# A two-layer graph network on one core: two weights are loaded later, the last pair is finished by halves of the features, and all end places are new

## The chip, the cores and the metric

The kernel runs on one core of a Trainium2 chip. A core has five engines that take their instructions in order, each from a queue of its own: TensorE (PE, matmuls), VectorE (DVE), ScalarE (ACT), GpSimd (POOL) and SyncE (SP, which here only issues DMAs). They meet through semaphores. The metric is the device time of one execution in microseconds (us).

## The reference

```python
x: (128 graphs, 128 nodes, 512 features), adj: (128, 128), all float32
# layer 0
q, k, v = (x @ Wq + bq, x @ Wk + bk, x @ Wv + bv), each in 8 heads of 64
scores = q @ k^T / sqrt(64) + (1 - adj) * -1e9
x = layernorm(x + softmax(scores) @ v @ Wo + bo)
# layer 1
h = x @ W;  s1 = h @ a1;  s2 = h @ a2
e = leaky_relu(s1[:, None] + s2[None, :], 0.2) * adj
h_prime = softmax(e) @ h
x = layernorm(x + elu(h_prime + beta * h))
```

Both norms have no scale and no shift of their own. The graphs do not touch each other.

## The kernel before

**Tiling.** The 128 graphs are taken two at a time: 64 pairs (G = 2, NG = 64), graph b0 and b1 of pair g. A pair brings 2 x 128 rows of 512 features. Everything is float32, and each matmul shows as two records in the trace.

**Block products.** q, k, v, w (the product with Wo) and h (the product of layer 1) are 2 x 2 block products done with seven block products instead of eight: `product(name, g, n)` with n from 1 to 7 (L269). It needs sums of weight blocks, made once by `weight_sum` (L207, on DVE for q and k, on POOL for v, w and h), and differences of data blocks for each pair, made by `block_sum` on POOL (L238). Products 1, 6, 5 and 3 go on in the same half of a PSUM bank (the main region), one on top of the other; 2 has the other half; 7 and 4 go to a side bank. After each of 1, 6, 5 and 3 `take_part` copies the state out (ACT for q, k, v and h, DVE for w), and the next product into that half waits for it. `add_block` (DVE) adds product 2, and the states after 7 and 4, to what take_part left. A block product of q or k is 4 matmuls of 128 columns, one of v, w or h 2 matmuls of 256 columns.

**Stages of a pair.** fetch_blocks and turn_x (DVE transposes x), block_sum x, q and k, scores (PE), mask (DVE), row_max (DVE), exps (ACT), row_inv, normalise (ACT), attn_write and attn_read (through DRAM, SP), turn_attn (DVE), v, attend (PE), attend_evict (ACT), w with the residual (x + bo, made by `residual` on POOL), the norm (bn_stats, bn_aggr, add_eps on DVE, inv_std on POOL), s1 and s2 by row_product (DVE), edge, leaky, edge_max, edge_exp, edge_inv, weights (the tile att), weights_write and weights_read through DRAM, weights_turn, aggregate (PE, tile pz), aggregate_evict (ACT, tile zT), h, then elu_max, elu_exp, elu_sum (u = max(h, 0) + x1, then + min(exp(h), 1)), the norm of layer 1, store. The -1 of elu falls away in the norm.

**The order is written out.** Nothing is scheduled by a tool. `rows(g)` (L685) gives every operation of a pair a place in us; pair g's places are shifted by g * STEP (36.678). `last_rows(g)` (L759) has the lists of the last two pairs; the table `other` has own places for pairs 0 to 3, NG - 4 and NG - 3. All pieces are sorted by place and emitted in that order, so the places decide only the order within each engine's queue, SP's and POOL's too:

```python
with tc.manual_schedule():
    for _, _, fn, args in sorted(pieces, key=lambda p: p[:2]):
        fn(*args)
```

Several pairs are under way at once: the operations of a pair spread from place -44 to 134.

**The start.** At the very beginning SP issues the blocks of pair 0, then wq, wk and wv (1 MB each, `load_turned`, L99), then, as their places come, the blocks of pair 1, the rows of x, wo and w1 (`load_weight`, L121). The biases, adj, a1, a2, beta and bo come on POOL's queue. `keep_busy(20, "early")` (L139) sets 20 idle products with the identity at the head of PE's queue.

**The end.** The last pair does w and h without block sums: `plain` (L323) does four matmuls of 512 columns into a bank for each graph; for this the free halves of wq_sb and wk_sb are loaded again with half of wo and of w1 (`load_again`). Six idle products ("late") stand in its list. Per graph follow elu_exp (ACT, L645), elu_max (DVE, L649), elu_sum (L654), bn_stats (L464), bn_aggr (L472), add_eps (L486), inv_std (POOL, L490), shift (L658), norm_f (ACT, L664) and store (L670), all over 512 features. The tile u has two buffers (`uf`).

## Time and profile before

| | |
|---|---|
| median of three runs | 2392.12 us (2390.34 to 2392.55) |
| the profiled execution | 2389.93 us |
| its span, first to last instruction | 2388.1 us |
| mean granted clock of PE | 0.997 |
| DMA traffic | 269.82 MB, 113 GB/s on average |
| wq, wk, wv landed at | 9.61, 12.99, 17.80 us |
| blocks of pair 1 landed by | 22.44 us |
| rows of x for pair 0 landed at | 22.4 and 23.12 us |
| last matmul ends at | 2379.43 us |

A share of busy time is a mean over the whole span. The table of windows gives the same by stretch of time: where PE is busy for the whole of a window, PE sets the pace there; where it isn't, the table of waits says what ended its pauses. A pause of another engine costs nothing by itself. The granted clock is a column of that table too: 1.00 is full speed. DVE's row of work in the page:

```profile
L387 DVE TENSOR_REDUCE nmax<-s 128x8 f32<-128x1024 f32 x128 | 153.5, 1199 | 2.3
L379 DVE SCALAR_TENSOR_TENSOR s<-psc,amask 128x512 f32<-128x512 f32 x256 | 167.6, 676 | 27.6 <-PE psc L371 27.3
L341 ACT COPY h<-ph 128x256 f32<-128x256 f32 x252 | 94.6, 376 | 258.4 <-PE ph L293 257.1
```

After the bar stand the busy sum, the mean duration of one in ns, and the idle time of the engine ahead of these instructions with what ended it.

### The profile page before, as it was taken

The page shows a single profiled execution, that of the slowest core. Times are in us where ns is not written, and L with a number is a line of the kernel's source. Part 1 is how long each engine was busy: PE and PEld are TensorE (multiplying, and loading weights), DVE is VectorE, ACT ScalarE, POOL GpSimd, SP SyncE. Part 2 cuts the span into 40 slices and gives each one's busy share as a digit, 9 for nine tenths or more (in the row PEclk, how much of TensorE's full clock was granted, in tenths as well). Part 3 has the DMA queues.
Part 4 walks back from the last instruction along what each step waited for, and adds up shares of the span by engine and source line. Part 5 has one row for each costly group of instructions (what it writes and reads, how often), then busy time and mean ns, then how long its engine had stood idle before and what let it go on. Part 6 is the DMA issues. An engine that isn't in the chain of part 4 may idle for free.

```text
span 2388.1 us, 50634 instructions
## 1 busy us (share of the span) xinstructions
PE 2359.0 (99%) x17708; PEld 2179.7 (91%) x17708; DVE 1876.4 (79%) x4381; ACT 1583.2 (66%) x5760; POOL 867.2 (36%) x1047
## 2 busy tenths in 40 slices
PE   8999999999999999999999999999999999999998
PEld 7898999999999999999999999999999999999985
DVE  6787787877877877878778778778788787787877
ACT  4676766766666666667666676676676666766655
POOL 6242433433433334334334333343343343333421
PEclk9999999999999999999999999999999999999999
DMA  6333334344343343343433433433434334334332
GB/s 191 103 95 115 108 104 132 92 120 124 101 119 114 103 125 105 106 132 93 120 121 103 119 112 105 125 100 111 133 91 120 117 107 118 107 111 125 118 100 73
DMA packets 255905, 269.82 MB, mean 113 GB/s; under 512 B 57425, under 2 KB 204369, under 8 KB 255265
## 3 DMA queue, kind: packets, MB, share of 16 engines
q1 hardware_dynamic: 254704, 265.45, 37.0%
q8 instruction: 140, 2.29, 0.4%
q14 instruction: 117, 0.95, 0.1%
q0 software_dynamic: 400, 0.86, 0.1%
q10 hardware_dynamic: 544, 0.26, 0.0%
HBM read 157.62 MB, written 108.85 MB: 112 GB/s over the span
## 4 chain that ended last, share of the span: by engine, by line
PE 95%; DMA 2%; DVE 1%; ACT 1%; SPq 0%; issue 0%; DVEq 0%; ACTq 0%
PE pv L293 12%; PE pk L299 12%; PE pq L299 11%; PE pw L293 11%; PE ph L293 11%; PE eq L299 9%; PE psc L371 5%; PE po L446 5%; PE pz L634 5%; PE ew L293 4%; PE ev L293 4%; PE eh L293 4%; DMA scr<-sb 1%; ACT sb L407 1%; DMA ab<-scr 1%; DMA wk_sb<-in_L_gnn_Wk_dram 0%
## 5 line engine op out<-in xcount | busy, mean ns | idle before, releaser
L393 ACT ACTIVATE s<-s,nmax 128x128 f32<-128x128 f32 x1024 | 398.1, 395 | 150.1 <-DVE nmax L387 150.1
L427 POOL TENSOR_TENSOR x<-x,bo_b_in 128x512 f32<-128x512 f32 x128 | 163.8, 1280 | 892.6 <-DMA x<-in_x_dram 769.9
L407 ACT ACTIVATE sb<-s,rinv 128x128 f32<-128x128 f32 x1024 | 319.5, 395 | 2.9 <-DMA scr<-sb 2.6
L347 ACT ACTIVATE kT<-pk,bk_c 128x128 f32<-128x128 f32 x512 | 160.6, 367 | 194.1 <-PE pk L299 151.5
L341 ACT COPY h<-ph 128x256 f32<-128x256 f32 x252 | 94.6, 376 | 258.4 <-PE ph L293 257.1
L347 ACT ACTIVATE qT<-pq,bq_c 128x128 f32<-128x128 f32 x512 | 159.2, 364 | 89.7 <-PE pq L299 89.3
L393 ACT ACTIVATION_READ_ACCUMULATOR s<-s,nmax 128x1 f32 x1024 | 196.9, 192 | 0.0
L252 POOL TENSOR_TENSOR th<-zT,zT 128x256 f32<-128x256 f32 x63 | 46.3, 736 | 395.5 <-ACT zT L641 395.5
L379 DVE SCALAR_TENSOR_TENSOR s<-psc,amask 128x512 f32<-128x512 f32 x256 | 167.6, 676 | 27.6 <-PE psc L371 27.3
L344 DVE TENSOR_TENSOR w<-pw,x 128x256 f32<-128x256 f32 x252 | 103.2, 410 | 101.0 <-PE pw L293 100.9
L497 DVE SCALAR_TENSOR_TENSOR ya<-w,wa_row 128x512 f32<-128x512 f32 x256 | 177.6, 694 | 4.4
L436 DVE STREAM_TRANSPOSE attnT<-ab 128x512 f32<-128x512 f32 x256 | 172.6, 694 | 7.4 <-DMA ab<-scr 6.5
L458 ACT ACTIVATE oT<-po,bv_c 128x128 f32<-128x128 f32 x512 | 139.6, 382 | 27.7 <-PE po L446 27.7
L387 DVE TENSOR_REDUCE nmax<-s 128x8 f32<-128x1024 f32 x128 | 153.5, 1199 | 2.3
L232 DVE STREAM_TRANSPOSE xT<-xblk 128x512 f32<-128x512 f32 x128 | 143.1, 1120 | 5.2 <-DMA xblk<-in_x_dram 5.2
L299 PEld LDWEIGHTS pk<-xT,wk_sb 128*128 128x128 f32 x1024 | 136.0, 195 | 10.6 <-issue 4.2
L299 PE MATMUL pk<-xT,wk_sb 128*128 128x128 f32 x1024 | 136.9, 278 | 4.1 <-DMA wk_sb<-in_L_gnn_Wk_dram 4.1
L293 PE MATMUL pv<-wv_sb,xT 128*128 128x256 f32 x512 | 137.6, 391 | 0.0
L299 PE MATMUL pq<-xT,wq_sb 128*128 128x128 f32 x1024 | 134.8, 275 | 0.0
L299 PEld LDWEIGHTS pq<-xT,wq_sb 128*128 128x128 f32 x1024 | 129.4, 192 | 3.3
L371 PE MATMUL psc<-kT,qT 64*128 64x128 f32 x2048 | 131.8, 278 | 0.0
L371 PEld LDWEIGHTS psc<-kT,qT 64*128 64x128 f32 x2048 | 119.4, 188 | 11.5 <-issue 11.3
(674 smaller groups left out, 6297.0 us busy)
## 6 DMA issues: line engine op xcount, KB each, us to landing
scr<-sb SPq DMA_DIRECT2D x128, 512.0 KB
ab<-scr SPq DMA_DIRECT2D x512, 128.0 KB
x<-in_x_dram SPq DMA_DIRECT2D x128, 256.0 KB
out_dram<-u SPq DMA_DIRECT2D x128, 256.0 KB
xblk<-in_x_dram SPq DMA_DIRECT2D x254, 128.0 KB
pb<-s2d SPq DMA_DIRECT2D x62, 128.0 KB
attd<-att SPq DMA_DIRECT2D x62, 128.0 KB
ab<-attd SPq DMA_DIRECT2D x248, 32.0 KB
```

Source lines behind the costliest of these rows:

```text
L232: nc.vector.transpose(xT[g][:, :, t * N : (t + 1) * N].rearrange("p m (b r) -> p b m r", r=Q), xblk[g][:, t].rearrange("p b (c m) -> p b m ...
L293: nc.tensor.matmul(out, b[:, c, :], a[:, c, :], start=first and c == 0, stop=(c == 1), skip_group_check=True,)
L299: nc.tensor.matmul(out[:, m * N : (m + 1) * N], a[:, c, m * P : (m + 1) * P], b[:, c, :], start=first and m == 0 and c == 0, stop=(c == 1) ...
L347: nc.scalar.activation(dst[:, m, :], src[:, m * N : (m + 1) * N], AF.Identity, bias=BIAS[name][:, 2 * i + m : 2 * i + m + 1],)
L371: nc.tensor.matmul(psc[b][j][:, m, :], qT[g][feats, m, rows], kT[g][feats, m, rows], start=True, stop=True,)
L379: nc.vector.scalar_tensor_tensor(s_t[b][:, j * HP : (j + 1) * HP, :], psc[b][j], SCALE, amask.rearrange("p (o n) -> p o n", o=1).broadcast ...
L387: nc.vector.tensor_reduce(nmax[b], s_t[b], AX.X, ALU.max, negate=True)
L393: nc.scalar.activation(s_t[b][:, h, :], s_t[b][:, h, :], AF.Exp, bias=nmax[b][:, h : h + 1], accum_out=rsum[b][:, h : h + 1],)
L407: nc.scalar.mul(sb[b][:, :, h, :], s_t[b][:, h, :].rearrange("p (b c) -> p b c", c=Q), rinv[b][:, h : h + 1],)
L427: nc.gpsimd.tensor_tensor(xr[b], xr[b], later["bo"], ALU.add)
L436: nc.vector.transpose(attnT[b].rearrange("p h (a r) -> p a h r", r=Q)[:, rows], ab[b].rearrange("p a (h c) -> p a h c", c=Q)[:, rows],)
L497: nc.vector.scalar_tensor_tensor(z, y[b], 1.0, wa_row[j], ALU.mult, ALU.mult, accum_out=s12[g][:, i, j : j + 1])
```

## The change

There are three parts.

1. **Start.** wk and wv are no longer issued right behind wq. A piece `load_k_and_v` stands at place 5.685, between the two turns of pair 0's x (5.683 and 6.713). Its memset of one column of wk_sb on DVE gives wk's DMA something on DVE to wait for, so that it issues behind the first turn. In pair 0 the q products stand ahead of the k products (before: k first), and DVE makes q's weight sums ahead of k's. w1 is loaded ahead of wo (before: behind), the rows of x of pair 0 ahead of the blocks of pair 1. There are 15 early idle products instead of 20.
2. **End.** In the last pair, layer 1's product, elu, statistics, norm and store work on halves of 256 features: half 1 ahead of half 0. The statistics of both halves go into one tile and are aggregated together; half 0 is normed by ACT, half 1 by DVE; there are four stores of 128 KB instead of two of 256 KB. The late idle products are gone. In the list of the last pair, graph b0's edges, weights, aggregate and product run ahead of b1's edge_max.
3. **Places.** All places are new: those of the steady pairs in rows(g), of the last two pairs, of the pairs in `other`, and of the single pieces at the start. The operations of a steady pair are the same, STEP too; in each queue their order is another. Among them, in a steady pair: row_max of b1 now stands ahead of add_block v 2 (before behind it), and take_part v 6 stands behind that add in both; the tile v is the same. residual of b0 stands ahead of the scores, before behind them. The number of matmuls that compute something does not change (halves apart: 16 of 256 columns instead of 8 of 512 in the last pair).

```diff
     load_turned(wq_sb, wq)
-    load_turned(wk_sb, wk)
-    load_turned(wv_sb, wv)
...
-    keep_busy(20, "early")
+    keep_busy(15, "early")
...
+    def load_k_and_v():
+        nc.vector.memset(wk_sb[:, 0, :1], 0.0)
+        load_turned(wk_sb, wk)
+        load_turned(wv_sb, wv)
...
+    def half(i):
+        return slice(i * HF, (i + 1) * HF)
+
+    def end_product(b, i):
+        pl["h", b, i] = ps_mm.tile([P, HF], F32, tag="mm", name=f"plh_{b}_{i}")
+        for c in range(NC):
+            nc.tensor.matmul(
+                pl["h", b, i], zT[b][:, c, :], (wk_sb if c < 2 else w1_sb)[:, c, half(i)],
+                start=(c == 0), stop=(c == NC - 1),
+            )
+
+    def end_exp(b, i):
+        nc.scalar.activation(whole("h", b)[:, half(i)], pl["h", b, i], AF.Exp)
+
+    def end_max(b, i):
+        if b not in u:
+            u[b] = wk2.tile([P, D], F32, tag="uf", name=f"u_{b}")
+        nc.vector.scalar_tensor_tensor(
+            u[b][:, half(i)], pl["h", b, i], 0.0, x1[b][:, half(i)], ALU.max, ALU.add
+        )
+
+    def end_sum(b, i):
+        nc.vector.scalar_tensor_tensor(
+            u[b][:, half(i)], hp[b][:, half(i)], 1.0, u[b][:, half(i)], ALU.min, ALU.add
+        )
+
+    def end_stats(b, i):
+        if b not in stats:
+            stats[b] = st.tile(
+                [P, 2, nc.vector.BN_STATS_DIM], F32, tag="stats2", name=f"stats2_{b}"
+            )
+        nc.vector.bn_stats(stats[b][:, i, :], u[b][:, half(i)])
...
+    def end_norm(b, i):
+        g, j = divmod(b, G)
+        dst, scale, bias = u[b][:, half(i)], rstd["f", g][:, j : j + 1], nmr[g][:, j : j + 1]
+        if i == 0:
+            nc.scalar.activation(dst, dst, AF.Identity, bias=bias, scale=scale)
+        else:
+            nc.vector.tensor_scalar(dst, dst, scale, bias, ALU.mult, ALU.add)
+
+    def end_store(b, i):
+        nc.sync.dma_start(out=out[b][:, half(i)], in_=u[b][:, half(i)])
...
     def rows(g):
...
-            (2.943, scores, b1), (3.203, product, "v", g, 1), (3.463, mask, b0, 0),
-            (3.487, mask, b0, 1), (3.658, row_max, b0), (4.555, exps, b0, 0),
-            (5.075, mask, b1, 0), (6.271, residual, b0), (6.383, product, "v", g, 2),
-            (6.541, exps, b0, 1), (7.568, take_part, "v", g, 1, 0, 0), (7.611, exps, b0, 2),
-            (8.122, product, "v", g, 7), (8.183, mask, b1, 1), (8.41, product, "v", g, 6),
-            (8.797, exps, b0, 3), (8.894, add_block, "v", g, 2, 0, 0),
-            (8.955, take_part, "v", g, 6, 1, 0), (9.854, row_inv, b0),
...
-            (11.052, row_max, b1), (11.513, normalise, b0, 3), (11.654, attn_write, b0),
-            (11.776, product, "v", g, 5), (12.497, exps, b1, 0), (13.24, exps, b1, 1),
...
+            (2.487, scores, b0), (3.199, scores, b1), (4.193, mask, b0, 0),
+            (4.492, product, "v", g, 1), (4.517, mask, b0, 1), (4.517, row_max, b0),
+            (4.641, mask, b1, 0), (5.302, take_part, "v", g, 1, 0, 0), (5.86, exps, b0, 0),
+            (6.834, residual, b1), (7.227, product, "v", g, 6), (7.65, product, "v", g, 2),
+            (7.788, exps, b0, 1), (8.282, mask, b1, 1), (8.312, exps, b0, 2),
+            (8.356, row_max, b1), (9.38, exps, b0, 3), (9.64, product, "v", g, 7),
+            (9.91, add_block, "v", g, 2, 0, 0), (10.078, take_part, "v", g, 6, 1, 0),
+            (10.336, row_inv, b0), (10.432, normalise, b0, 0), (10.446, normalise, b0, 1),
+            (10.513, normalise, b0, 2), (11.118, product, "v", g, 5), (12.165, normalise, b0, 3),
...
     def last_rows(g):
...
-            (43.463, keep_busy, 6, "late"), (43.587, weights, g, 0), (44.057, edge_max, g, 1),
...
-            (48.603, plain, "h", b0), (48.733, aggregate_evict, b1), (52.053, plain, "h", b1),
-            (53.543, elu_exp, b0), (55.613, elu_max, b0), (55.743, elu_exp, b1),
...
+            (46.907, aggregate_evict, b0), (47.677, end_product, b0, 1),
+            (49.407, end_product, b0, 0), (49.557, edge_max, g, 1), (49.647, end_exp, b0, 1),
...
+            (51.747, turn_weights, g, 1), (52.187, weights_evict, g, 1), (52.707, aggregate, b1),
+            (53.237, end_exp, b0, 0), (53.847, aggregate_evict, b1),
+            (54.617, end_product, b1, 1), (54.847, end_max, b0, 0), (55.207, end_max, b0, 1),
...
+            (58.317, end_max, b1, 0), (58.317, end_exp, b1, 0), (58.677, end_aggr, b0),
...
-    at(7.47, weight_sum, "k", 3, nc.vector)
...
-    at(10.35, weight_sum, "q", 3, nc.vector)
...
+    at(5.685, load_k_and_v)
+    at(8.723, weight_sum, "q", 3, nc.vector)
...
+    at(13.163, weight_sum, "k", 3, nc.vector)
```

## The prediction

> **What bounds the kernel now.** I read the page's busy line and chain first, then the table of windows for where TensorE (PE) stands still, then the waits of PE for what ends each pause, then the last microseconds, and last a stretch of VectorE's (DVE's) timeline in the middle.
>
> ```profile
> PE 2359.0 (99%) x17708; PEld 2179.7 (91%) x17708; DVE 1876.4 (79%) x4381; ACT 1583.2 (66%) x5760; POOL 867.2 (36%) x1047
> ...
> PE 95%; DMA 2%; DVE 1%; ACT 1%; SPq 0%; issue 0%; DVEq 0%; ACTq 0%
> ```
>
> PE is the bound. The diff adds and removes no real matmul, so only PE's pauses, its slow clock and what follows its last matmul can change.
>
> ```profile
> 0.00:20.00 20.00, 12.47 (x79) 12.15 (x80) 9.10 (x12) 2.54 (x5) 10.81 (x23) 0.91 0.93 264
> 200.00:220.00 20.00, 17.84 (x104) 16.20 (x103) 16.21 (x41) 16.32 (x62) 9.56 (x13) 0.94 0.32 111
> 1000.00:1100.00 100.00, 100.00 (x761) 92.70 (x761) 80.19 (x192) 69.90 (x257) 39.89 (x48) 1.00 0.33 102
> 2270.00:2290.00 20.00, 16.96 (x146) 15.60 (x146) 12.07 (x25) 7.76 (x27) 1.67 (x3) 0.91 0.21 66
> 2380.00:2388.10 8.10, 0.00 (x0) 0.00 (x0) 3.29 (x10) 1.69 (x3) 1.08 (x2) 0.61 0.17 65
> ```
>
> Columns: window, its length, busy time of PE, weight loads, DVE, ACT, POOL, then PE's granted clock, DMA share, GB/s. The middle is full (100 of 100); pauses lie in the first 100 us, near 217, near 2275, in the last pair and after the last matmul.
>
> ```profile
> PE pk L299 <- DMA wk_sb<-in_L_gnn_Wk_dram: 4.1, 1, 4.1
> PE ph L293 <- ACT h L341: 3.4, 4, 2.2
> PE pk L299 <- ACT kT L347: 3.0, 2, 1.9
> PE early L137 <- POOL ident masks.py:199: 2.7, 1, 2.7
> PE pq L299 <- ACT qT L347: 2.5, 1, 2.5
> ```
>
> ```profile
> 2379.53 0.61 ACT h L645
> ...
> 2384.22 0.81 ACT u L664
> ```
>
> Each wait line has the sum, how often, the longest (early is the idle product at the start). 4.1 us go by until wk is there; 2.5 (at 2279) and 2.2 (at 217) are single pauses. The two lines of the second fence are from the chain that ends last (start, us): behind the last matmul come exp at 2379.53, the norm at 2384.22, and the end at 2388.07.
>
> ```profile
> 1002.36 0.42 DVE L357 TENSOR_TENSOR kT<-eq,kT 128x256 f32<-128x256 f32 x1 [0.20 <-PE eq L299]
> 1002.70 0.42 DVE L357 TENSOR_TENSOR qT<-eq,qT 128x256 f32<-128x256 f32 x1
> 1003.03 1.13 DVE L232 STREAM_TRANSPOSE xT<-xblk 128x512 f32<-128x512 f32 x1
> 1004.08 0.12 DVE L608 RECIPROCAL einv<-esum 128x2 f32<-128x2 f32 x1
> 1004.24 0.77 DVE L615 SCALAR_TENSOR_TENSOR att<-ee,einv,beta_i 128x128 f32<-128x128 f32 x2
> 1005.34 1.29 DVE L379 SCALAR_TENSOR_TENSOR s<-psc,amask 128x512 f32<-128x512 f32 x2 [0.33 <-PE psc L371]
> 1006.66 1.22 DVE L387 TENSOR_REDUCE nmax<-s 128x8 f32<-128x1024 f32 x1
> 1007.80 1.11 DVE L232 STREAM_TRANSPOSE xT<-xblk 128x512 f32<-128x512 f32 x1
> ```
>
> Start, duration, instruction: from one start to the next I take what a DVE step occupies in a full queue (xT 1.05, nmax 1.14).
>
> **What the Trainium skill says.** "TensorE: Matmul & The Clock Gate", Part 1, has a free-running activity window of about 3.4 us; idleness halves the clock until the array has been busy again. The trace agrees: after 4.1 us of pause, 13.1 to 16.7 runs at clock 0.50, and the 16 matmul records there take 3.57 us against 1.79 later. After 2.1 us at 51 the clock stays 1.00 (40 to 60), after 2.3 and 2.6 it falls (0.94 and 0.91 above): the border lies near 2.3 us here. "SBUF — State Buffer", section "SBUF: two separate sides", says that a DVE operation with two SBUF inputs and a GpSimd one exclude each other for the whole instruction. The trace agrees: at 238.17 the second att (0.35 alone) takes 0.82, because POOL's tw, started at 238.06, ends at 238.84. "DMA: Bandwidth & Descriptors", "Queues, rings and completion order", has descriptors of a ring consumed in order; here wq, wk and wv land at 9.61, 12.99 and 17.80, as issued.
>
> **The change part by part.**
>
> *Start.* wk and wv now issue behind the first turn of x (about 6.3 instead of 2.15 and 2.63). wq needs until 9.6 to land and wk follows in the same ring, so I take wk at 13.1, as before. What changes is that q, whose weights are there at 9.6, goes first: three q products (4 matmuls of 128 columns at 0.223, so 0.89 each) = 2.7 us lie in what was pause, and PE no longer meets wk after 4.1 us of idleness, so the half clock (3.57 - 1.79 = 1.8) goes. 15 idle products instead of 20 end near 7.0 (records come at 6 to 7 per us until 6.0, then 11 to 12); that leaves 2.6 us until wq, at the border of the clock. Should it halve there, the q products end near 15 instead of 12.3; of that 1.9 at most falls behind wk. The other pauses before 100 us sum to 1.0 + 2.1 + 1.2 + 0.4 + 0.9 = 5.6. For the new order I laid its instructions one after another, engine by engine, with the durations of the same rows here and the measured steps between engines: pk behind ACT's kT 0.4; pair 1's first product behind the turn of its blocks, which land at 23 because the x rows stand ahead of them on SP, 1.7; 0.7; and 0.9 near 48 behind k's add: 3.7. Together 2.7 + 1.8 + 1.9 = 6.4 at best; 2.5 if the clock halves and the blocks land 2 us later. I take 4.5. The DVE memset of one column is under 0.1 and lies in DVE's pause before the weights. The swap of w1 and wo moves 1 MB transfers that are needed after 30: nothing, under pair 0's attention; 1.2 by the same laying-out if both land 2 us later.
>
> *Near 217 to 240.* Before: pauses of 2.3 + 0.3 + 0.4, and a clock of 0.94 over 20 us, 1.2: 4.2. New order: 1.1 (217), 0.4, 0.9 (236), 1.4 (239), 3.8, each below the border. Gain 0.3; -1.0 if the last two together lower the clock.
>
> *The steady pairs.* Nothing to gain (no pause). What can be lost: the fifth v product, which goes on in the bank that ACT empties, waits for take_part of the sixth; that stands behind DVE's add of the second v product (same v tile), now queued behind both row_max. From k's last add on, DVE never rests. In steps of the timeline: kT 0.34, qT 0.33, turn 1.04, einv 0.03, turn 1.05, two att with a block_sum of POOL between them 0.98 (1.01 from 237.90 to 238.91), two masks 1.32, row_max 1.12, mask 0.59, w 0.45, w add 0.34, mask 0.72, row_max 1.12, v add 0.42; then ACT 0.03 + 0.37 and 0.05 to PE: 10.3. PE's way from the same eq matmul (DVE reads it 0.42 after its start) to the fifth v product: 0.32, 16 po at 0.119, 16 psc at 0.124 (means, with the changes of shape), 16 of 256 columns at 0.432 and one change of 0.10 = 11.2, less 0.42 = 10.8. Some 0.5 is left (0.35 to 0.6 by roundings), against 0.24 measured for the tightest wait of the steady pairs now. I cost it at nothing; each 0.1 missing would cost 6 us over about 58 pairs. All other margins come out at 0.9 or more; those of DVE for attn_read's landings at 2.0.
>
> *2240 to 2340.* Before: 0.6 + 0.7 + 2.6 + 0.8 + 0.3 = 5.0 of pause, and a clock of 0.91 over 20 us, 1.8: 6.8. New order: 0.2, 0.9, 0.2. I allow 0.5 for late DMAs: gain 5.0, 3.0 if one pause of 2 us stays.
>
> *Last pair.* Before: 0.8 + 1.1 + 0.4 + 0.4 = 2.7 of pause and 1.3 of idle products, 4.0. Now one graph's chain runs whole ahead of the other's, so each product h waits for its own z (0.42 from the last aggregate to ACT and some 0.6 of evict): 1.1 and 0.8; before them 0.4 each behind attT, and 1.3 on the way: 4.0. Eight matmuls of 256 columns (0.43) for four of 512 (0.86) are even. With what may stand in a queue, a loss of 0.5.
>
> *Tail.* Before: from the end of the last matmul (first record 2378.41 + 0.86) to 2388.07, 8.8. Now, halves estimated from the 128x256 rows: 0.2 to ACT and DVE, max 0.42 beside exp 0.37, sum 0.42, bn_stats 0.45, aggregate 0.21, eps 0.18, POOL's pow 0.62, shift 0.19, ACT's norm 0.60, store 2.06, to the span's end 0.98: 6.3. Gain 2.5; the same queues carry b0's work, so 2.0, and 0.5 if each half costs what a whole does.
>
> *What the laying-out misses.* Done for the old order, it shows 0.0 of pause in the middle, as the trace does, but lacks some 3 us of single pauses outside (0.8 "issue" at 75, 0.8 near 100, 0.5 near 2320, 0.7 in the last pair). Such ones will be in the new order too: -2.5.
>
> Sum: 4.5 + 0.3 + 0 + 5.0 - 0.5 + 2.0 - 2.5 = 8.8. Of the profiled 2389.93 that leaves 2381.1; of the median 2392.12, which lies 2.2 above it, 2383.3. I take the median's.
>
> **Rivals.** (a) *Start and end trade places*: xblk_1 sets when pair 1 runs and the 2.6 us pause halves the clock (start 1.0, not 4.5), and one long pause near 2275 stays (3.0, not 5.0): 8.8 - 3.5 - 2.0 = 3.3, so 2388.8, no change that can be told. For it: DMA share 0.93 in the first 20 us, and a single 2 us pause appears twice in the old order. Against: q's 2.7 us lie in idleness for certain. (b) *Slower: the v chain in every steady pair.* Place: second att and both row_max ahead of v's add; POOL has a second block_sum queued right behind the first, and if it too goes before att, the chain is 0.73 longer, 0.23 beyond the margin: 58 x 0.23 = 13, so 2396.6. It decides from 0.15 beyond the margin. For it: att at 967.2 took 1.28 behind a POOL operation of 1.27. Against: at 238.84 the waiting att went ahead of the tw that was queued (0.77 long, begun 238.80). (c) *Halves save nothing*: twice the instructions at their fixed costs, tail 0.5: 2384.8, inside the forecast's range.
>
> **How the numbers follow.** Forecast with (c) 0.75, (a) 0.13, (b) 0.12. About 0.2% (4.8 us) is what a measurement of this kernel tells from no change. The forecast's own range, from its bounds (start 2.5 to 6.4, 2240 on 3.0 to 5.5, tail 0.5 to 2.5, misses 0 to -5), is 2380 to 2387.5. With (a) taken in whole: 2379.5 to 2390. Faster: nearly all of the forecast and a little of (a), 0.75; same: most of (a) and an edge of the forecast, 0.13; slower: (b), 0.12.
>
> **What would show it.** Right: no wait on wk above 1 us, q products from 9.6 on, clock 1.00 around 2280, 6.3 to 6.8 behind the last matmul, the middle at 100 of 100. Wrong: among the waits of PE a line of pv behind ACT's v with some 58 entries; 9 us there undo everything. A clock below 1 at 10 to 13, or over 2 us of pause in one piece after 2240, would say (a).

## The result, and the profile after

| | before | after |
|---|---|---|
| median, taken together on one chip | 2390.45 us (2390.21 to 2392.55, 6 runs) | 2380.51 us (2378.62 to 2381.36, 6 runs) |
| the profiled execution | 2389.93 us | 2381.36 us |
| its span | 2388.1 us | 2379.6 us |
| mean granted clock of PE | 0.997 | 0.998 |
| wq, wk landed at | 9.61, 12.99 us | 11.06, 16.25 us |

The ratio of the runs is 0.9955, with an interval of 0.9943 to 0.9968: the change is faster by 9.9 us (7.6 to 13.6 by the interval). The two profiled executions lie 8.6 us apart. From the page after:

```profile
PE 2353.9 (99%) x17702; PEld 2177.3 (91%) x17702; DVE 1960.5 (82%) x4390; ACT 1589.5 (67%) x5762; POOL 867.7 (36%) x1047
...
PE 95%; DMA 2%; DVE 1%; ACT 1%; issue 0%; SPq 0%; POOLq 0%; POOL 0%; ACTq 0%; DVEq 0%
```

PE is the bound as before. From its waits (sum, how often, the longest), and from two tables of windows (columns as in the prediction):

```profile
PE pq L304 <- DMA wq_sb<-in_L_gnn_Wq_dram: 3.0, 1, 3.0
...
PE pk L304 <- DMA wk_sb<-in_L_gnn_Wk_dram: 2.1, 1, 2.1
...
PE pb L533 <- DVE s_in L510: 1.6, 1, 1.6
PE plh L668 <- ACT zT L646: 1.6, 2, 0.9
```

```profile
1000.00:1100.00 100.00, 100.00 (x742) 92.77 (x739) 84.11 (x190) 69.61 (x254) 38.56 (x47) 1.00 0.35 108
2270.00:2290.00 20.00, 19.28 (x161) 17.55 (x160) 17.18 (x35) 13.08 (x55) 6.16 (x8) 1.00 0.15 33
```

```profile
8.00:10.00 2.00, 0.20 (x2) 0.01 (x1) 0.00 (x0) 0.94 (x1) 1.84 (x4) 1.00 0.56 139
10.00:12.00 2.00, 0.80 (x7) 0.83 (x8) 0.88 (x2) 0.34 (x1) 0.60 (x1) 1.00 0.81 314
12.00:14.00 2.00, 2.00 (x19) 1.99 (x18) 1.89 (x3) 0.62 (x2) 0.00 (x0) 1.00 1.03 422
14.00:16.00 2.00, 0.20 (x2) 0.01 (x1) 0.62 (x2) 0.00 (x0) 0.00 (x0) 1.00 1.01 420
16.00:18.00 2.00, 1.70 (x10) 1.71 (x11) 1.66 (x3) 0.00 (x0) 0.00 (x0) 0.73 0.98 387
18.00:20.00 2.00, 2.00 (x12) 2.00 (x11) 1.25 (x3) 0.43 (x2) 0.00 (x0) 0.50 1.14 192
20.00:22.00 2.00, 2.00 (x18) 2.00 (x18) 0.00 (x0) 0.81 (x3) 0.34 (x1) 0.91 1.13 204
```

The middle is still full, and the stretch around 2280 is no longer slow: 19.28 of 20 busy at clock 1.00, against 16.96 at 0.91. The start is not what I had laid out. 8.2 to 11.2 is a pause (wq is late), 14.2 to 16.3 another (wk is late), and from 16.9 to 20.3 PE runs at half the clock.

To see where the 8.6 us come from, I gave every matmul its cost, and compared the times at which the two executions had done the same amount of PE's work (idle products left out):

| up to (us before) | gain so far | the part gains |
|---|---|---|
| 120 | 3.4 | 3.4 |
| 281 | 3.6 | 0.2 |
| 2251 | 4.1 | 0.5 |
| 2341 | 9.7 | 5.6 |
| end of the last matmul | 7.4 | -2.3 |
| end of the span | 8.5 | 1.1 |

So in this pair of executions the places near the end bring most, the start brings a good third, and the last pair, which the change reshaped by hand, gives back more than the shorter tail earns.

For the start one pair of executions is too few. At 120 us this one and six others with the same start and the same loads, from the runs below, stand 3.4 to 7.0 us ahead of the profiled kernel before, 4.8 in the mean; the four with the old start lie between 3.1 behind it and 2.3 ahead, 1.0 behind in the mean. My estimate from these means is 5.7 or 5.8 us for the start. It rests on eleven single executions, so it is rough.

### The profile page after: what moved, and what is told of

It is laid out like the page before. It is cut to its first block, busy times and chain, and to the rows that moved or that the text cites. A ratio compares the mean times of both kernels' runs of the same rounds, so it can differ in the third digit from the quotient of the medians.

```text
span 2379.6 us, 50867 instructions
## 1 busy us (share of the span) xinstructions
PE 2353.9 (99%) x17702; PEld 2177.3 (91%) x17702; DVE 1960.5 (82%) x4390; ACT 1589.5 (67%) x5762; POOL 867.7 (36%) x1047
## 4 chain that ended last, share of the span: by engine, by line
PE 95%; DMA 2%; DVE 1%; ACT 1%; issue 0%; SPq 0%; POOLq 0%; POOL 0%; ACTq 0%; DVEq 0%
PE pk L304 12%; PE pq L304 12%; PE pv L298 12%; PE ph L298 11%; PE pw L298 11%; PE eq L304 9%; PE psc L376 5%; PE po L451 5%; PE pz L639 5%; PE eh L298 4%; PE ew L298 4%; PE ev L298 4%; DMA w_sb<-in_L_gnn_W_dram 1%; DMA wk_sb<-in_L_gnn_Wk_dram 0%; DMA scr<-sb 0%
## 5 line engine op out<-in xcount | busy, mean ns | idle before, releaser
L412 ACT ACTIVATE sb<-s,rinv 128x128 f32<-128x128 f32 x1024 | 325.2, 392 | 0.4 <-DVE rinv L405 0.4
L502 DVE SCALAR_TENSOR_TENSOR ya<-w,wa_row 128x512 f32<-128x512 f32 x256 | 223.9, 874 | 4.4
L346 ACT COPY v<-pv 128x256 f32<-128x256 f32 x256 | 94.4, 369 | 86.4 <-PE pv L298 59.9
L257 POOL TENSOR_TENSOR tx<-xT 128x256 f32<-128x256 f32 x128 | 95.6, 748 | 124.3 <-PE psc L376 104.3
L654 DVE SCALAR_TENSOR_TENSOR u<-h,x 128x512 f32<-128x512 f32 x126 | 87.1, 691 | 63.7 <-ACT h L346 61.6
L304 PEld LDWEIGHTS pk<-xT,wk_sb 128*128 128x128 f32 x1024 | 130.2, 193 | 5.5 <-DMA wk_sb<-in_L_gnn_Wk_dram 2.3
```

The lines of the kernel that those rows point to most:

```text
L304: nc.tensor.matmul(out[:, m * N : (m + 1) * N], a[:, c, m * P : (m + 1) * P], b[:, c, :], start=first and m == 0 and c == 0, stop=(c == 1) ...
L346: nc.scalar.copy(dst, src)
L412: nc.scalar.mul(sb[b][:, :, h, :], s_t[b][:, h, :].rearrange("p (b c) -> p b c", c=Q), rinv[b][:, h : h + 1],)
L502: nc.vector.scalar_tensor_tensor(z, y[b], 1.0, wa_row[j], ALU.mult, ALU.mult, accum_out=s12[g][:, i, j : j + 1])
```

## The experiments

Unless said otherwise a kernel computes the same as the changed one. Its gain or loss "in the trace" is taken at equal work of PE, as in the table above.

### The start

**Before's start in the changed kernel.** The single pieces of the start and the places of pairs 0 to 3 (`rows_a`) are those of the kernel before:

```diff
-    keep_busy(15, "early")
+    load_turned(wk_sb, wk)
+    load_turned(wv_sb, wv)
+    keep_busy(20, "early")
...
+    FIRST = 4
...
-        own = rows(g) if g < NG - 2 else last_rows(g)
+        first = g < FIRST
+        own = (rows_a(g) if first else rows(g)) if g < NG - 2 else last_rows(g)
...
-    at(5.685, load_k_and_v)
```

> The changed kernel with the start of the kernel before: pairs 0 to 3 with their old places, the old single pieces, loads and 20 idle products; steady pairs and end are the changed ones. If the start is worth the 3.6 us that the two traces show between the first matmul and 280 us, this costs that and what the seam between the two orders (pairs 3 and 4) adds, which by laying out the order is 3 to 4 us of pauses between 140 and 250: 2384 to 2389. If the gain of the start is only an effect of the steady order, it stays at 2380 to 2382.

Measured: 2391.4 us (2389.17 to 2394.3, 13 runs), ratio to before 1.0003 (0.9995 to 1.0011), slower than I had expected. All of the gain is gone. The profiled execution is the slowest of the 13; PE's clock is 0.50 in it from 13.1 to 23.3. In the trace it falls 4.2 us behind the changed kernel by 60 us, and then 8.7 more by 231, where pairs in the old order meet pairs in the new one: 10.9 us by the medians is more than the start itself is worth. Its waits of PE between 100 and 260:

```profile
PE pv L300 <- ACT v L348: 3.1, 3, 1.4
PE ph L300 <- ACT h L348: 2.7, 3, 1.8
```

**The start alone in the kernel before.** Start, places of pairs 0 to 3 and single pieces are the changed kernel's; all the rest is old. The edit mirrors the last one, upon the kernel before:

```diff
-    load_turned(wk_sb, wk)
-    load_turned(wv_sb, wv)
...
+        own = (rows_a(g) if first else rows(g)) if g < NG - 2 else last_rows(g)
...
+    at(5.685, load_k_and_v)
```

> The kernel before with the changed start alone (pairs 0 to 3, single pieces, later wk and wv, 15 idle products); steady pairs and the end as before. Theory: the gain up to 280 us of 3 to 4 us stays and nothing else comes: 2386 to 2388. The pause of 2.6 us near 2279 with its slow clock is still there. Rival (phase: the stall near 2279 goes when the start shifts): 2382 or less.

Measured: 2383.28 us (2381.18 to 2385.9, 5 runs), ratio 0.9967 (0.9954 to 0.9979), more than I had expected. In the trace it is 4.6 us ahead of before from 256 on, keeps 5.1 through the middle and ends 4.4 ahead. The medians say 7.9, the traces 4.5. The profiled executions make that difference: the one of before lies 1.2 below the median of its 25 runs here, this kernel's 2.1 above its own. The long pause near the end is still there, with 0.91 as the mean clock from 2270 to 2290:

```profile
PE pq L304 <- ACT qT L352: 2.3, 1, 2.3
```

So it isn't the new start that takes this pause away. Which of the moved places near the end does wasn't tried.

**The end alone in the kernel before.** Places from pair 60 on and the last pair by halves are the changed kernel's; pairs up to 59 (`rows_a`) and the start are old:

```diff
+    FIRST = NG - 4
...
+        first = g < FIRST
+        own = (rows_a(g) if first else rows(g)) if g < NG - 2 else last_rows(g)
```

> The kernel before with the changed places from pair 60 on and the end by halves; start and steady pairs as before. Theory: the end is worth 5.5 - 2.1 + 1.0 = 4.4 by the traces; the seam between the two orders (pairs 59 and 60) costs some 2.5 us near 2190 to 2230 and one pause of about 2.3 near 2273, so 2388 to 2391. Rival (the end's gain needs no steady order of its own): 2385 to 2386.5.

Measured: 2392.5 us (2388.92 to 2395.96, 13 runs), ratio 1.0006 (0.9998 to 1.0014). In the trace it is 2.8 us behind before at 60 already, with before's own start (wk came at 14.51); that is chance. Then it loses 6.2 us between 2187 and 2260, where the old steady order meets the new places, and wins 4.3 behind 2277. So the parts don't add: an order of the last pairs fits the steady order that it was made for. What the end is worth in the changed kernel I read from its trace (5.6), not from this run.

**wk and wv early again.** The only edit to the changed kernel: the two loads stand right behind wq's again.

```diff
+    load_turned(wk_sb, wk)
+    load_turned(wv_sb, wv)
...
-    at(5.685, load_k_and_v)
```

> The changed kernel with wk and wv issued right behind wq again; all else of the change stays, q first among it. Theory A (the later issue costs time: in the changed kernel the DMA share falls to 0.56 between 8 and 10 us, wq lands at 11.1 and wk at 16.3 instead of 9.6 and 13.0, and PE stands 2.1 us at wk): wq at 9.6, wk at 13.0, the wait on wk below 1 us, no half clock at 18 to 20, everything from there on 2 to 3 us earlier, so 2377.5 to 2378.5 against the changed kernel's 2380.5. Rival B (pair 1's blocks and POOL's small loads set the pace, which is why the loads were moved): wk lands earlier, but the pause moves behind the turn of pair 1's blocks, time within 0.7 us of the changed kernel. Rival C (small loads on POOL's queue come later beside the big ones): 2381 or more.

Measured: 2380.13 us (2377.66 to 2381.1, 5 runs), ratio 0.9949 (0.9937 to 0.9962): no difference to the changed kernel's 2380.51. wk landed at 14.06, the wait for it shrank to 0.4 and the clock stayed at 1.00; in its place stands one wait on DVE's turn of pair 1's blocks:

```profile
PE pk L306 <- DVE xT L239: 1.3, 1, 1.3
```

In the trace it is 1.7 us ahead until 256, then 0.5, and -0.5 from 2000 on. That lead is no gain of the early issue: two executions that issue wk late (the one by wholes and the one with its own u tile, both below) are 1.7 ahead until 256 as well. Issuing wk and wv later therefore brings nothing that these runs can tell. What the start brings must lie in its order, but no run has k ahead of q with all else new, so which part of the order brings it is not shown.

**Pair 1's blocks first.** Upon the last kernel: the blocks of pair 1 ahead of the rows of x on SP, and the stores of the halves 0 issued by ACT.

```diff
-            16.888, 17.781, 17.638, 6.483, 18.771, 18.531, 18.531, 21.043, 20.317, 16.823, 21.45,
+            16.888, 17.781, 17.638, 6.73, 18.771, 18.531, 18.531, 21.043, 20.317, 16.823, 21.45,
...
-            -23.195, -17.695, -16.665, -10.045, -9.265, -4.965, -7.205, -13.682, -10.048,
+            -29.958, -17.695, -16.665, -10.045, -9.265, -4.965, -7.205, -13.682, -10.048,
...
-        nc.sync.dma_start(out=out[b][:, half(i)], in_=u[b][:, half(i)])
+        (nc.scalar if i == 0 else nc.sync).dma_start(out=out[b][:, half(i)], in_=u[b][:, half(i)])
```

> The changed kernel with wk and wv issued right behind wq, the blocks of pair 1 ahead of the rows of x in SP's queue, and the half-0 stores of the last pair issued by ACT instead of SP. With early loads alone the time stayed (2380.1) and a wait of 1.3 us on the turn of pair 1's blocks took the place of the wait on wk. Theory (the landing of pair 1's blocks sets the start): they land 1.5 to 2 us earlier, that wait goes, 1 us is won, and the last store issues 0.4 us earlier: 2378.5 to 2379.2. Rival (POOL's residual, which needs the rows of x, and the weight sums behind it in POOL's queue come later and stop PE elsewhere): 2380 or more.

Measured: 2379.04 us (2378.32 to 2382.14, 5 runs), ratio 0.9954 (0.9941 to 0.9968), not told from the changed kernel. The wait on the turn is gone, and 2.4 us of waiting for DVE's k before the first scores have come instead. ACT's stores change nothing: 7.7 us behind the last matmul, as with SP.

### The steady pairs

**A longer chain to v's add.** The sum of elu and the statistics of b0 stand ahead of DVE's add of v in every steady pair, instead of behind:

```diff
-            (107.63, elu_exp, b1), (120.701, elu_sum, b0), (120.887, bn_stats, u, b0, "f"),
+            (107.63, elu_exp, b1), (119.8, elu_sum, b0), (119.9, bn_stats, u, b0, "f"),
```

> The changed kernel with two DVE operations of every steady pair (elu_sum and bn_stats of b0, about 1.2 us from start to start in a full queue with the wait between them) moved ahead of the second v product's add. In the changed trace the fifth v product has 0.42 to 0.5 us left behind ACT's copy. Theory (the margin is real and each us beyond it is paid in every pair): the waits of PE show pv behind ACT's v some 54 times, 0.7 to 0.8 each, 38 to 44 us in all: 2418 to 2425. Rival (DVE or PE make it good in the slack of the rest of the pair, since DVE is busy 82%): under 2390.

Measured: 2446.41 us (2445.73 to 2447.09, 2 runs), ratio 1.0231 (1.0212 to 1.025): slower, and by more than I had expected. Its waits of PE; then, in one pair there and in one of the changed kernel, DVE's second turn of x, the sum of elu and the add of v; between the two, the GpSimd line that the sum meets in the longer chain:

```profile
PE pv L298 <- ACT v L346: 55.3, 56, 1.1
```

```profile
1021.45 1.09 DVE L237 STREAM_TRANSPOSE xT<-xblk 128x512 f32<-128x512 f32 x1
...
1029.17 1.01 DVE L659 SCALAR_TENSOR_TENSOR u<-h,u 128x512 f32<-128x512 f32 x1
...
1030.82 0.41 DVE L362 TENSOR_TENSOR v<-pv,v 128x256 f32<-128x256 f32 x1
```

```profile
1028.90 0.73 POOL L257 TENSOR_TENSOR tx<-xT,tx 128x256 f32<-128x256 f32 x1
```

```profile
1000.03 1.10 DVE L237 STREAM_TRANSPOSE xT<-xblk 128x512 f32<-128x512 f32 x1
...
1007.76 0.42 DVE L362 TENSOR_TENSOR v<-pv,v 128x256 f32<-128x256 f32 x1
...
1008.74 0.68 DVE L659 SCALAR_TENSOR_TENSOR u<-h,u 128x512 f32<-128x512 f32 x1
```

From the second turn of x to v's add (start to start) the chain takes 9.37 us instead of 7.73, 1.64 more: 1.04 for the sum, 0.61 for the statistics. I had expected some 1.2. The sum took 1.01 here since GpSimd's tx (1028.90 to 1029.63) lay across its start; in its old place it took 0.68. That is the exclusion which the Trainium skill describes ("SBUF — State Buffer", "SBUF: two separate sides"): it makes an operation with two SBUF inputs dearer in one place than in another. In this pair the fifth v product starts 8.23 us behind the first, in the changed kernel 7.02: 1.21 later, so 1.64 - 1.21 = 0.43 of margin was there. In the changed kernel's own trace that product starts 0.46 us or more behind the end of ACT's copy in every pair from 7 to 61, 0.49 in the median; 0.06 of that passes even where PE waits, in the longer chain, which leaves 0.40 and 0.43.

### The clock near 2280

**The kernel before, kept warm.** Eight idle products stand ahead of the q product that waits near 2279:

```diff
+    at((NG - 2) * STEP + -4.724, keep_busy, 8, "warm")
```

> The kernel before with eight idle products (about 1.8 us) put into PE's queue ahead of the product of q that waits 2.6 us near 2279; nothing else differs. In the trace of before PE's clock is 0.50 from 2279.4 to 2282.7. Theory (the pause itself lowers the clock, which costs 1.65 us behind it): the clock stays 1.00 there and 1.6 us are won, 2389 to 2390 against 2391.2, and in the trace from the waiting product to the end. Rival (the clock falls for another reason, or the idle products only delay the waiting product): no gain, 2391 to 2392.

Measured: 2388.91 us (2385.46 to 2392.53, 21 runs) beside 2390.9, ratio 0.9993 (0.9986 to 0.9999). A microsecond of the windows and the waiting product with the next two, in the kernel before and in this one, whose trace is 2.8 us ahead there:

```profile
2280.00:2281.00 1.00, 1.00 (x6) 1.00 (x6) 1.00 (x3) 0.14 (x1) 0.00 (x0) 0.50 0.00 0
```

```profile
2279.41 2.08 PE L299 MATMUL pq<-xT,s_q 128*128 128x128 f32 x8 [2.47 <-ACT qT L347]
2281.28 1.80 PE L299 MATMUL pk<-xT,s_k 128*128 128x128 f32 x8
2282.92 1.06 PE L299 MATMUL eq<-tx,wq_sb 128*128 128x128 f32 x8
```

```profile
2277.00:2278.00 1.00, 1.00 (x12) 1.00 (x11) 1.00 (x3) 0.53 (x3) 0.00 (x0) 1.00 0.00 0
```

```profile
2276.67 1.16 PE L299 MATMUL pq<-xT,s_q 128*128 128x128 f32 x8 [0.75 <-ACT qT L347]
2277.66 1.06 PE L299 MATMUL pk<-xT,s_k 128*128 128x128 f32 x8
2278.65 1.16 PE L299 MATMUL eq<-tx,wq_sb 128*128 128x128 f32 x8
```

A window can be busy for its whole length and still do little more than half of the work: from the start of pq to that of eq the same two products take 3.51 us at clock 0.50 and 1.98 at 1.00. With what the idle products delay, the kernel gains 1.3 us in the trace and keeps them to the end. So of the changed kernel's 5.6 us in this stretch, 1.3 are the clock (2279.4 to 2282.8 at half speed would give 1.7), and the rest are pauses that are gone.

### The last pair and the tail

**The last pair by wholes.** The changed kernel, with layer 1 and norm of the last pair over 512 features again (plain, elu_exp, elu_max, elu_sum, bn_stats, norm_f, store in the places of the halves):

> The changed kernel with the last pair's layer-1 product, elu, statistics, norm and stores on all 512 features again, in the same order of the graphs (b0 ahead of b1); late idle products stay out. Theory: the halves shorten what follows the last matmul, by 1.0 in the traces (7.75 against 8.8 from its end to the span's end), so this costs 1.0 to 2.0: 2381.5 to 2382.5, with 8.8 or more behind the last matmul. Rival: the halves pay twice the fixed costs and the gain of the tail came from the new order alone: 2380 to 2381, tail under 8.

Measured: 2380.49 us (2378.64 to 2382.38, 5 runs), ratio 0.9955 (0.9943 to 0.9968): the halves make no difference that can be told. In the traces it takes 21.6 us from the same product (eh of pair 62, the last one that both kernels do alike) to the end, with halves 20.9: 0.75 for the halves.

**The second graph's softmax early.** In the change, b0's chain runs whole before b1's edge_max. Here b1's edge_max, edge_exp, edge_inv and weights stand ahead of the norm of pair 62, and its turn and aggregate between b0's products:

```diff
-            (49.407, end_product, b0, 0), (49.557, edge_max, g, 1), (49.647, end_exp, b0, 1),
-            (50.027, edge_exp, g, 1), (50.697, edge_inv, g, 1), (51.077, weights, g, 1),
-            (51.747, turn_weights, g, 1), (52.187, weights_evict, g, 1), (52.707, aggregate, b1),
-            (53.237, end_exp, b0, 0), (53.847, aggregate_evict, b1),
+            (49.407, end_product, b0, 0), (44.3, edge_max, g, 1), (49.647, end_exp, b0, 1),
+            (45.1, edge_exp, g, 1), (45.8, edge_inv, g, 1), (45.85, weights, g, 1),
+            (46.0, turn_weights, g, 1), (46.95, weights_evict, g, 1), (48.5, aggregate, b1),
+            (53.237, end_exp, b0, 0), (49.7, aggregate_evict, b1),
```

> The changed kernel with one thing moved: in the last pair the second graph's edge softmax (its maximum, exp, reciprocal, weights) stands ahead of the norm of the pair before on DVE and ACT, and its weights' turn and aggregate stand on TensorE (PE) between the products of the first graph's halves, instead of behind both. In the changed kernel's trace PE waits in that stretch 0.36 and 0.35 us behind attT, 0.90 and 0.68 behind zT. If these waits are what the last pair lost (my reading of why its term came out at -2.2 and not at -0.5), the second two go, the last matmul ends 1.0 to 1.4 us earlier after the same place, and the tail behind it stays at 7.7: a span shorter by some 1.2, median about 2379.3, at the edge of what runs can tell. Rival: DVE has the norm of the pair before still to do, so the tail behind the last matmul grows by as much as PE gains: no difference to the changed kernel.

Measured: 2379.42 us (2378.44 to 2381.9, 5 runs), ratio to before 0.9953 (0.9939 to 0.9966). PE's timeline (start, busy, and in brackets its idle time before, with what ended it), first in the changed kernel, then here:

```profile
2360.22 1.16 PE L639 MATMUL pz<-attT,x 128*128 128x128 f32 x8 [0.36 <-ACT attT L629]
2362.28 1.13 PE L668 MATMUL plh<-wk_sb,zT 128*128 128x256 f32 x4 [0.90 <-ACT zT L646]
...
2366.46 1.16 PE L639 MATMUL pz<-attT,x 128*128 128x128 f32 x8 [0.35 <-ACT attT L629]
2368.29 1.13 PE L668 MATMUL plh<-wk_sb,zT 128*128 128x256 f32 x4 [0.68 <-ACT zT L646]
```

```profile
2358.76 1.16 PE L639 MATMUL pz<-attT,x 128*128 128x128 f32 x8 [0.35 <-ACT attT L629]
2360.23 0.30 PE L626 MATMUL pat<-ident,att 128*128 128x128 f32 x1 [0.32 <-DVE att L620]
2360.82 1.13 PE L668 MATMUL plh<-wk_sb,zT 128*128 128x256 f32 x4 [0.28 <-ACT zT L646]
```

From eh (the last product of pair 62 on PE) to the end of the last matmul PE needs 11.45 us instead of 13.12, as theory had it. But the tail behind it grows from 7.75 to 9.18, so the rival is right about the time: 0.24 is left in the trace, and the medians can't tell it from the changed kernel. DVE's timeline tells why. The first maximum of the last pair (elu of b0, both halves), here and in the kernel before all changes:

```profile
2367.20 0.76 DVE L679 SCALAR_TENSOR_TENSOR u<-plh,x 128x256 f32<-128x256 f32 x2 [3.00 <-DMA out_dram<-u]
```

```profile
2378.15 0.69 DVE L649 SCALAR_TENSOR_TENSOR u<-plh,x 128x512 f32<-128x512 f32 x1 [3.00 <-DMA out_dram<-u]
```

DVE stands idle for 3.0 us, and what lets it go is the landing of a store: u has two buffers, and the last pair's take those of pair 62. Only when pair 62's output has been written may DVE begin.

**A tile of its own for the last pair.** `tag="uf"` becomes `tag="ul"` in end_max, alone in the changed kernel and then together with the early softmax:

```diff
-            u[b] = wk2.tile([P, D], F32, tag="uf", name=f"u_{b}")
+            u[b] = wk2.tile([P, D], F32, tag="ul", name=f"u_{b}")
```

> The changed kernel with one edit: the last pair's tile u has two buffers of its own and no longer takes those of the pair before. In the changed kernel's trace DVE's first maximum of the last pair starts at 2368.29, though both halves of its product are there at 2365.8; the store of the pair before, which reads the same buffer, lands at 2368.20. If the buffer is what held it, it starts near 2366 now. Worth to the time: little, since DVE is idle again 0.47 us ahead of the next graph's maximum at 2371.09, which waits for ACT's exp: 0 to 0.4 us, median 2380.1 to 2380.5. Rival: nothing changes in DVE's times, then it wasn't the buffer.

Measured: 2380.37 us (2379.9 to 2380.9, 5 runs), ratio 0.9956 (0.9943 to 0.997). The first maximum, in the changed kernel and here:

```profile
2368.29 0.76 DVE L679 SCALAR_TENSOR_TENSOR u<-plh,x 128x256 f32<-128x256 f32 x2 [2.64 <-ACT zT L646]
```

```profile
2366.33 0.76 DVE L679 SCALAR_TENSOR_TENSOR u<-plh,x 128x256 f32<-128x256 f32 x2 [1.77 <-ACT h L674]
```

This execution is 1.10 us ahead of the changed kernel's through the whole last pair, so 2368.29 - 1.10 - 2366.33 = 0.86 of it is the buffer: that held it. The changed kernel's line names ACT's copy of z instead, which ended at 2368.24, 0.04 behind the landing of the store: where two things end together, the list names the later one. The tail is 7.75 as without the edit: alone it is worth nothing.

> The same edit upon the kernel whose second graph's edge softmax runs early. There the last matmul ended 1.67 us earlier, but the tail behind it took 9.18 instead of 7.75, and DVE stood idle for 3.0 us before its first maximum until a store had landed. If that buffer bounds the end, the maximum starts near 2365.4 instead of 2367.2, DVE has no queue left when the last product is done, and the tail is 7.4 to 7.75 again: a span shorter by 1.4 to 1.8 than without the edit, 3 below the changed kernel's for the same start; median 2377 to 2378. Rival: the tail stays above 9, since the last graph's own operations on DVE and ACT take that long.

Measured: 2378.28 us (2377.05 to 2379.99, 5 runs), ratio 0.9947 (0.9935 to 0.996), the lowest median of all. The first maximum:

```profile
2367.47 0.76 DVE L679 SCALAR_TENSOR_TENSOR u<-plh,x 128x256 f32<-128x256 f32 x2 [1.85 <-ACT h L674]
```

It waits for ACT's exp of the same half now, and starts 1.15 us earlier against the same matmuls than without the edit; not 1.8, since the product of that half had only just ended. The tail is 8.06, so the end after eh is 1.4 us shorter than the changed kernel's. By the traces, two edits of which each alone is worth 0 to 0.2 us are worth 1.4 together: each took away one of two waits that ended at about the same time. The medians lie 2.2 us below the changed kernel's, but the two intervals overlap, so the runs alone don't show it.

**All together.** The early softmax (without the own tile), the early loads, pair 1's blocks first, and ACT's stores.

> The same move, together with the early loads of wk and wv, the blocks of pair 1 ahead of the x rows, and the stores of the first halves issued by ACT. If the parts add up: start some 1 to 2 us better than the changed kernel's profile, end 1.2 better: 2377.5 to 2378.5. Rival: the early gain is taken back at the seam near 256 us as before, and the end's too: 2379 to 2380.5.

Measured: 2380.43 us (2379.14 to 2380.92, 5 runs), ratio 0.9954 (0.9942 to 0.9967): the parts do not add up, as the rival says. At 281 us its trace is 0.4 ahead of the changed kernel, with a half clock from 11.1 to 14.5, and the tail is long again; the run has no u tile of its own.

## Why the prediction was right

**The sum** was 8.8 us. The profiled executions differ by 8.6, the medians by 9.9. The forecast median, 2383.3, came out 2.8 too high, 1.7 of it because the three runs of before from which I started had a median of 2392.12 and the six measured beside the change 2390.45. Seen term by term it is less good: three terms came out as worked out, the start was near its size by another way than mine, two were mis-sized, and the allowance at the end paid for them.

- **Start, 4.5; measured 3.4 at 120 us** (5.7 or so by the means of several executions). The size holds, the working doesn't. I took wq at 9.6 and wk "at 13.1, as before", because it "follows in the same ring". Here wq landed at 11.06 and wk at 16.25, and in six other executions that issue wk as late it landed at 14.29 to 16.05, against 12.54 to 14.51 in six that issue it early. Redone from the waits: the first product begins at 11.20 instead of 13.12, 1.9 earlier; the wait on wk takes 2.1 of that back; the half clock, which I had struck out, came back and costs the same in both; and the pauses from there to 110 us sum to 1.7 (0.9, 0.4 and 0.4) where before has 5.2. That makes 3.3. So the gain is the 3.5 of the later pauses, for which I had put 1.9, and not q's 2.7 and the clock's 1.8: two errors that cancel, and luck. Which move took those pauses away is open.
- **217 to 240, 0.3; measured 0.2.** About as worked out: 2.9 are won up to 231 and 2.7 lost by 281, and the clock stays at 1.00. The price of the old clock was too low: I read it from a window that ends at 220, but the half clock lasts from 217.8 to 221.2 and costs 1.7, not 1.2.
- **The steady pairs, 0; measured 0.5.** The 0.5 is a single delay of the profiled execution of before, which the other runs gain too, the warmed kernel with before's own order among them. Right with its reason. I had 0.5 us of margin for the fifth v product (0.35 to 0.6); read from the trace it is 0.43 in the median, and the longer chain gives 0.43 too. Rival (b) needed POOL's second sum to go ahead of att as well; with 0.40 left at the least in pairs 7 to 61, that didn't come to bear. The longer chain shows that its price was real, and not too high. Before's own 0.5 is the same thing once: at 967 a residual of POOL (1.27 us) lies across att, which takes 2.01 us for its two parts instead of 1.09, the sum of elu behind it takes 1.16 instead of 0.68, and at 976.5 a v product that waits for ACT's copy of v starts 0.5 us late.
- **2240 to 2340, 5.0; measured 5.6.** Right, the clock too: the warmed kernel gains 1.3 where I had put down 1.8. That the pauses would go is shown; which move took away the one of 2.5 us is not.
- **The last pair, -0.5; measured -2.3.** The pauses behind z and attT were nearly as listed (0.90, 0.68, 0.36, 0.35 against 1.1, 0.8, 0.4, 0.4). Mis-sized was "1.3 on the way": it was 2.6, 1.6 of it in one wait of pb for s_in, which in executions of the same places came out at 0.4 to 1.7. The traces tell where that comes from: s_in of pair 62 stands in DVE's queue behind two turns of pair 63's attention, and these wait for the way through DRAM. In the changed kernel the write of that attention took 4.98 us and PE waited 1.6; in the kernel by wholes, with the same places up to there, 3.93 and 0.5.
- **The tail, 2.0; measured 1.05.** "6.3 to 6.8 behind the last matmul" was 7.75. I had put DVE's maximum "beside" ACT's exp; they read the same half of PSUM one after the other, and the maximum itself stood behind half 1's statistics. From the end of the last matmul to the end of both that is 1.3 us where I had 0.6. The four stores leave SP one by one, and the span ends 1.4 instead of 1.0 behind the last landing. From the changed kernel's timeline (SPq: the issuing of the four stores):

```profile
2372.35 0.41 DVE L679 SCALAR_TENSOR_TENSOR u<-plh,x 128x256 f32<-128x256 f32 x1
2372.79 0.38 ACT L674 ACTIVATE h<-plh 128x256 f32<-128x256 f32 x1 [1.74 <-DVE u L679]
...
2375.07 1.79 SPq L707 DMA_DIRECT2D out_dram<-u  x4
```

- **What the laying-out misses, -2.5.** This allowance was for single pauses that the old trace had and my laying-out lacked. The terms above, measured, leave nothing for it: 3.4 + 0.2 + 0.5 + 5.6 - 2.3 + 1.1 = 8.5. It stood in for the losses in last pair and tail (2.8 more than I had booked there), so the sum came out right: luck, since the allowance was meant for other pauses.

**The signs.** Of what was to show that I was right, two came (the clock at 1.00 around 2280, the middle at 100 of 100) and three did not: wk was waited for 2.1 us, q's products began at 11.2 and not at 9.6, and 7.75 us lie behind the last matmul.

**Rival (a)**, start and end trading places, is half seen: the long pause and the half clock at the start are there, the one near 2275 isn't. **Rival (c)**, halves save nothing, is what the runs say (2380.49 by wholes, 2380.51 by halves); the traces leave the halves 0.75 us.

Not settled: how much the start alone is worth. The trace of the kernel with the new start alone says 4.5 us, its medians 7.9 (by the interval, 5 to 11), the means of several executions at 120 us about 5.7. The loads of the start land up to 3.4 us apart in executions with the same loads in the same order: pair 1's last block came at 25.53 in the changed kernel and at 22.1 in the one with the longer chain.

## What to carry to other kernels

When a new order is laid out by hand, take the landing of a moved load as unknown by the spread that several executions show, and not at its old value; a wait that is taken away at the start gives its place to the next one. And don't take a term of the start from one pair of executions. At an end where two waits finish within a microsecond of each other (here a chain of softmax on PE's side, and a buffer held by the store of the pair before on DVE's), an edit to one of them measures as nothing: look at what every engine of the tail waits for, and take both away in one run before calling either worthless. Where two engines read one accumulator tile, count their times one after the other.

## What the runs showed of the hardware that I had not expected

- **What lowers the clock here is the idle part of a fixed window, and not the length of a pause.** In the changed kernel a pause of 3.0 us (8.2 to 11.2) left the clock at 1.00 and one of 2.1 us (14.2 to 16.3) was followed by 3.4 us at 0.50; the windows stand above. The clock's own records in the traces tell why. Every half clock ahead of a kernel's last matmul, in all fourteen traces, lasts 3.41 us or two or three times that, and within a trace they begin whole multiples of 3.413 us apart (before: 12.97, 217.77 and 2279.42). So I laid each trace out in windows of that length and summed PE's idle time in each. At full clock, 27 windows have 1.99 us or more of it, and the half clock follows all of them; some 9700 have 1.94 or less, and it follows none. It ended behind windows with up to 0.25 us of idleness and stayed behind those with 0.65 or more. The pause of 3.0 us fell into two windows, 1.9 and 1.1; that of 2.1 us lay within one. My "border near 2.3 us" was therefore wrong, and rested on a misreading too: the pauses at 51, 217 and 2279 are 1.9, 2.2 and 2.5 us. The free-running window of the Trainium skill ("TensorE: Matmul & The Clock Gate", Part 1) fits in its length, but the page lets the clock fall after a whole idle window, and here 2.0 us of 3.4 were enough. Where the windows lie against the kernel's start differs between executions, so a pause of 2.0 us or a little more may cost 1.7 us in one and nothing in the next: 2.07 us at 8.7 in the kernel with all moves brought the half clock, 2.35 us at 26.8 in the one with pair 1's blocks first did not.
- **Two engines that read the same PSUM tile took turns.** In both halves of the last graph, and in the kernel before with its 512 columns, the second of maximum and exp began 0.03 us after the first had ended, whichever came first. The Trainium skill says that two engines must not be on one bank in the same partitions at once, reads included ("PSUM — Partial Sum Buffer", Terms); the trace agrees: the second one waits for a semaphore of the first (1.74 us in ACT's line above), so the program keeps them apart, and each such pair costs the sum of both and not the longer one.
- **Four stores issued back to back by SP** leave 0.42 to 0.49 us apart. The last one left at 2376.46, though its data was ready at 2376.03.
